# Down products of two pairs of pages at once, and a new order of loads ahead of a layer's first x

## The chip, the cores and the metric

The kernel runs on one core of a Trainium2 chip. A core has a matrix engine (TensorE, PE in the profile; its weight loads are PEld), three engines that work on rows of numbers (VectorE or DVE, ScalarE or ACT, GpSimd or POOL), and SyncE (SP), which issues transfers. ACT and POOL issue transfers too, in the order of their own instructions. Each engine goes through its own queue in order, and waits there for semaphores that other engines or transfers raise. All transfers share 16 DMA engines. The metric is device microseconds from start to end of one execution; lower is better. All arithmetic here is in 32-bit floats but for a few helpers.

## The reference, cut to what matters

An input x of 4 x 1024 tokens of width 256 goes through four residual steps: RWKV attention, a mixture of experts, retention, and the same mixture again with the same weights.

```python
x = x + attn_a(layernorm(x), ...)      # RWKV
x = x + ffn(layernorm(x), router_w, router_bias, wg, wu, wd, swg, swu, swd)
x = x + attn_b(layernorm(x), ...)      # retention, 16 heads
x = x + ffn(layernorm(x), router_w, router_bias, wg, wu, wd, swg, swu, swd)
```

The mixture takes, for each token, 4 of 64 experts, and adds two shared ones that see every token:

```python
_, topk_idx = jax.lax.top_k(logits + router_bias, K)          # K = 4, E = 64
g = jax.nn.silu(jnp.einsum('nd,edf->nef', flat, wg))          # d = 256, f = 64
u = jnp.einsum('nd,edf->nef', flat, wu)
routed = jnp.einsum('ne,nef,efd->nd', comb, g * u, wd)
shared = jnp.einsum('nsh,shd->nd', sg * su, swd)
return (routed + shared).reshape(b, t, d)
```

## The kernel before, in words

The 4096 tokens are 8 segments of 512 (NSEG, SEG). Only the chosen experts' products are computed. For that, each token's normalised row is sent four times (L429, an indirect DMA by POOL) into `sent`, a table in DRAM that is cut into pages of 128 rows. A page belongs to one expert; `owner` says to which. Two pages make a pair. As long as the tokens spread as usual, the list USUAL says how many pairs hold all rows of the segments up to i: 33, 38, 43, 51, 59, 67, 75, 83. So each of the two mixture layers (objects `f1` and `f2`) works on 83 pairs, numbered 0 to 82.

`routed` (from L520) does a pair in steps, and step p of the layer calls them for different pairs:

- `load(p)`: reads the owners of the pair, loads x, 256 KB from `sent` (L530, tile rx), and the two experts' weights, 192 KB each from `wx` (L532, tile rw), all issued on SP.
- `up(p - 2)`: four transposes of x on PE (rt, L542) and one copy on DVE (rxT, L546).
- `mid(p - 3)`: eight matmuls for gate and up (rg, L554), Silu on ACT (rs, L559), the product on DVE (rh, L562), and ACT's copy of rh to the other 64 partitions (L563), so that both halves of the down product can read it.
- `down(p - 4)`: eight matmuls (rp, L574) into two PSUM banks, one for each half of the 256 columns, two evictions of 128x256 into ry (L581), and one write of 256 KB to `made` in DRAM (L582), issued on ACT. Pairs below 33 have the second half evicted by DVE, the others by ACT.

The buffers: rx and rw four deep in layer 1 and six in layer 2, ry two and four, rh two. The tags A, B and C of the PSUM banks have 4, 3 and 1 buffers; rt, rp and some others share B.

`gather` takes the products of a segment back: 16 indirect DMAs by POOL (gy, L606; 4 tiles of 128 tokens by 4 choices), and for each an addition on DVE, weighted by the router (L617). `gathers` puts a segment's fetches at the position until(i) + 3.5, spread over 8 steps, and its additions LAG = 7 steps later. A fetch names the rows of `made` that it may read: tile t of segment i reads up to pair until(i) + 2 t, and therefore waits for the writes of all pairs before that.

All work is written out as tracks of steps with positions, which `merge` (L54) sorts into one program order; the engines' queues follow from it. Positions of layer 1 count in pairs.

The stages: `stage_1` (to about 384 us) is RWKV, the routing of layer 1 and its sends. `first_layer` (from L1184) merges layer 1's routed pairs with retention (`stage_2`, from L824), four batches of 1024 tokens, the first from position until(0) + 14 = 47. When `stage_2` is called, it issues retention's loads: five weight matrices b_w (L833), seven small vectors (L837, L840, L841), and three loads from a table of decays (L858, L865), all on SP, ahead of the first pair's loads. `stage_2`'s pools `pb` and `pw` take over memory that stage 1's pool `pa` held, with the last segment's normalised rows in it, which the sends read. After layer 1, the rest of retention and the routing of layer 2 follow, then `second_layer`: layer 2's pairs merged with gathers, the shared experts and the stores of the output (L1253).

Of the kernel before, what the change touches and what calls it, by code (L numbers as in the profile page):

```python
# [10 lines left out]
F32 = mybir.dt.float32  # L11
BF16 = mybir.dt.bfloat16
# [48 lines left out]
def hybrid_kernel(ctx: ExitStack, tc: tile.TileContext, a: dict, out: bass.AP):  # L61
# [98 lines left out]

    PACE, LAG = 2, 7.0

# [80 lines left out]
    class Ffn:  # L243
# [5 lines left out]
        def __init__(self, name, pool, keep, deep):  # L249
            self.name, self.pool, self.keep = name, pool, keep  # L250

            self.deep = deep
            self.xnT, self.pick, self.turned, self.weights = {}, {}, None, None

            self.rows = (pool, 2)

            self.paced = False


            self.end, self.room = none, None  # L260
            self.upto = self.keep.tile([P, NSEG, E], F32, tag="upto", bufs=1, name=f"upto_{name}")
# [256 lines left out]
        def routed(self, pool, until):  # L518

            st, first, last = {}, until(0), until(NSEG - 1)  # L520

            def load(p):
                nm = f"{self.name}{p}"
                _, got = nc.values_load_multi_w_load_instructions(  # L524
                    self.owner[p : p + 1, :], engines=[SP], min_val=0, max_val=E - 1,
                    skip_runtime_bounds_check_because="place() counts at most E - 1 experts",
                )
                x = pool.tile([P, 2, D], F32, tag="rx", bufs=self.deep[0], name=f"rx_{nm}")
                w = pool.tile([P, 2, WD + P], F32, tag="rw", bufs=self.deep[0], name=f"rw_{nm}")
                nc.sync.dma_start(out=x, in_=sent[p * P : (p + 1) * P])  # L530
                for j, e in enumerate(got):
                    nc.sync.dma_start(  # L532
                        out=w[:, j], in_=wx[bass.ds(e, 1)].rearrange("e p c -> p (e c)")
                    )
                st[p] = dict(x=x, w=w)

# [12 lines left out]
            def mid(p):  # L549
# [10 lines left out]

                h = pool.tile([P, 2, P], F32, tag="rh", bufs=2, name=f"rh_{nm}")
                beat(nc.vector.tensor_mul(out=h[:F], in0=gu[F:], in1=act[F:]))  # L562
                nc.scalar.copy(out=h[F:], in_=h[:F])  # L563
                s["h"] = h

            def down(p):
                nm, s = f"{self.name}{p}", st.pop(p)
                y = pool.tile([P, 2, D], F32, tag="ry", bufs=self.deep[1], name=f"ry_{nm}")
                halves = [bank("B", f"rp_{nm}_{c}", [P, 2, P]) for c in range(2)]
                for j in range(2):  # L570

                    for c, yp in enumerate(halves):
                        r = slice(c * F, (c + 1) * F)
                        nc.tensor.matmul(  # L574
                            yp[:, j, :], lhsT=s["h"][r, j, :], rhs=s["w"][r, j, WD:],
                            start=True, stop=True,
                        )
                for c, yp in enumerate(halves):

                    copy = nc.vector.tensor_copy if c and p < first else nc.scalar.copy  # L580
                    copy(out=y[:, :, c * P : (c + 1) * P], in_=yp)  # L581
                nc.scalar.dma_start(out=made[p * P : (p + 1) * P], in_=y)  # L582

            def step(p):
                if p < last:
                    load(p)
                for d, f in ((2, up), (3, mid), (4, down)):
                    if 0 <= p - d < last:
                        f(p - d)

            return track([lambda p=p: step(p) for p in range(last + 4)], 0, last + 4)

# [33 lines left out]
        def gathers(self, pool, until):  # L626

            out = []
            for i in range(NSEG):
                at = until(i) + 3.5  # L630
                fetch, add = self.gather(i, pool, until)
                out += [track(fetch, at, at + PACE * TT), track(add, at + LAG, at + LAG + PACE * TT)]
            return out


    def stage_1(ctx: ExitStack, ffn, pf):
        pa = ctx.enter_context(tc.tile_pool(name="pa", bufs=1))
        rows = ffn.rows = (pa, 4)

# [184 lines left out]
    def stage_2(ctx: ExitStack):  # L824
        pb = ctx.enter_context(tc.tile_pool(name="pb", bufs=1))
        pw = ctx.enter_context(tc.tile_pool(name="pw", bufs=2))
        NQ = T // QS
        CPQ = QS // CH

        two = [wide(n, f"b_w{n}").rearrange("p (n k d) -> p n k d", n=2, d=D) for n in range(3)]  # L830
        wq, wk, wv, wg, wo = (two[n // 2][:, n % 2] for n in range(5))
# [4 lines left out]
        for n, t in cols.items():  # L836
            nc.sync.dma_start(out=t, in_=a[n])  # L837
        bv_bc = pb.tile([P, D], F32, name="bv_bc")
        bo_3 = pb.tile([3, D], F32, name="bo_3")
        nc.sync.dma_start(out=bv_bc, in_=a["bv"].partition_broadcast(P))  # L840
        nc.sync.dma_start(out=bo_3, in_=a["bo"].partition_broadcast(3))  # L841

        bo_rows = pb.tile([3, D], BF16, name="bo_rows")
        part = pw.tile([3, D], BF16, tag="bo_part", bufs=1, name="bo_part")
        sums = pw.tile([3, D], F32, tag="bo_sums", bufs=1, name="bo_sums")
        nc.vector.memset(sums, 0.0)
# [7 lines left out]
        with nc.allow_low_precision("each row is BF16"):  # L854
            nc.vector.tensor_copy(out=bo_rows, in_=sums)

        decay = pb.tile([P, H, CH], F32, name="decay")
        nc.sync.dma_start(  # L858
            out=decay,
# [4 lines left out]
        for k in range(KC):  # L864
            nc.sync.dma_start(  # L865
                out=qdec[:, k, :],
                in_=bass.AP(
                    tensor=tab.tensor, offset=tab.offset + k * HPB * W + Z + 1,
                    ap=[[W, HPB], [0, HD], [1, CH]],
                ),  # L870
            )
# [46 lines left out]
        def normed(b, s, what):  # L918
            xnT = pw.tile([P, KC, QS], F32, tag="xnTb", bufs=1, name=f"xnT_{what}{b}_{s}")
            tiles = [xtile(b, s * CPQ + t) for t in range(CPQ)]  # L920
            xn = layernorm(pw, tiles, f"{what}{b}_{s}")
            transposed(xn, CPQ, xnT, f"{what}{b}_{s}")
# [19 lines left out]
        def batch(b):  # L942
# [7 lines left out]
            def quarter(tag, s):  # L950
                return pb.tile([P, KC, QS], F32, tag=tag, bufs=NQ + 1, name=f"{tag}_{b}_{s}")

# [210 lines left out]
    pf = ctx.enter_context(tc.tile_pool(name="pf", bufs=2))  # L1163
    f1 = Ffn("f1_", pf, keep, (4, 2, 4))

# [18 lines left out]
    def first_layer(until):  # L1184

        arm, held = ExitStack(), ExitStack()
        f2 = Ffn("f2_", pf, arm.enter_context(tc.tile_pool(name="keep2", bufs=NSEG)), (6, 4, 6))

        first = until(0) + 14
        cut = until(NSEG - 1) + 4 + LAG + PACE * TT  # L1190
        with right("pr1") as pr, right("pg") as pg:
            batch = stage_2(held)
            batches = []
            for b in range(B):
# [3 lines left out]
            merge(  # L1198
                f1.routed(pr, until), *f1.gathers(pg, until), [s for s in batches if s[0] < cut]
            )  # L1200
# [45 lines left out]
    def second_layer(f2, pr, until):  # L1246
# [5 lines left out]
        for i in range(NSEG):  # L1252
# [5 lines left out]
            f2.routed(pr, until), *gathers, stores, track(side, 0.5, n - 4),  # L1258
            track(f2.shared(NSEG - 1), n - 3, n + 4 + LAG),
        )  # L1260
# [65 lines left out]
```

## Time and profile before

| what | us |
|---|---|
| median of 3 runs | 1428.38 (1427.42 to 1430.12) |
| profiled execution, its own time | 1426.64 |
| its span, first to last instruction | 1424.7 |
| PE busy | 1260.2 (88%) |
| DVE busy | 994.2 (70%) |
| ACT busy | 738.6 (52%) |
| POOL busy | 529.9 (37%) |
| evictions of the down products on ACT (x266) | 92.8 |
| last send of layer 1 issued / first x of layer 1 issued | 381.38 / 390.59 |
| first transpose on PE, layer 1 / layer 2 | 394.93 / 1107.43 |

The transfers move 276 MB, 194 GB/s over the span, very unevenly: 349 GB/s and more between 420 and 520 us, 55 GB/s between 800 and 1074. The shares above are averages over stages with different limits. So a stage is read by the windows of the profile, which give each engine's busy time, the clock granted to PE and the DMA engines' share in one stretch; a wait, by the engine that sat idle and what released it.

### The profile page before, as it was taken

What the parts mean: (1) busy time and instruction counts of PE and PEld (TensorE: products, weight loads), DVE (VectorE), ACT (ScalarE), POOL (GpSimd) and SP (SyncE); (2) the same over time, 40 slices, a digit from 0 to 9 for tenths busy, and PEclk for the clock granted to TensorE, in tenths of its full rate; (3) what the DMA queues carried; (4) which work ended last, traced back from release to release, by engine and by line L of the source; (5) the groups of instructions that cost most, each with busy time, mean ns of one, the idle gap of its engine ahead of it and who ended that gap; (6) DMA issues with size and microseconds to landing.
All of it is one profiled execution on the core that took longest, in us unless ns stands there. A gap on an engine that the chain in (4) does not pass through costs nothing. (4 is left out here: it accounts for less than half of the span.)

```text
span 1424.7 us, 23821 instructions
## 1 busy us (share of the span) xinstructions
PE 1260.2 (88%) x7872; PEld 891.4 (63%) x7872; DVE 994.2 (70%) x2510; ACT 738.6 (52%) x1422; POOL 529.9 (37%) x536
## 2 busy tenths in 40 slices
PE   6789999999389979998998999799997899999993
PEld 2455555556277767776776666566464687777772
DVE  6999989998355547775777788866673355486664
ACT  7989888973134455555654463433331234454440
POOL 0043255536400155432334105536717000376565
PEclk9999999999789999998999999799999899999997
DMA  9985931112399996765552101212202898999984
GB/s 350 403 254 74 297 115 60 60 37 82 123 310 349 336 331 211 235 206 195 164 187 91 36 31 68 74 38 79 100 16 103 260 318 278 324 384 378 363 310 128
DMA packets 192297, 276.26 MB, mean 194 GB/s; under 512 B 53795, under 2 KB 119718, under 8 KB 192166
## 3 DMA queue, kind: packets, MB, share of 16 engines
q1 hardware_dynamic: 143686, 163.98, 36.1%
q0 software_dynamic: 24576, 67.14, 14.2%
q10 hardware_dynamic: 23904, 43.53, 8.1%
q8 instruction: 65, 1.06, 0.3%
q14 instruction: 66, 0.54, 0.1%
HBM read 166.05 MB, written 121.11 MB: 202 GB/s over the span
## 5 line engine op out<-in xcount | busy, mean ns | idle before, releaser
L429 POOL DMA_INDIRECT sent<-xn_f,to_f x256 | 278.2, 1087 | 415.3 <-issue 192.9
L606 POOL DMA_INDIRECT gy_f<-made,to_f x256 | 248.6, 971 | 468.9 <-DVE rh_f L562 143.3
L554 PE MATMUL rg_f<-rxT_f,rw_f 128*128 128x128 f32 x1328 | 186.6, 283 | 8.4 <-DVE rxT_f L546 2.9
L554 PEld LDWEIGHTS rg_f<-rxT_f,rw_f 128*128 128x128 f32 x1328 | 165.9, 194 | 19.7 <-DVE rxT_f L546 11.6
L559 ACT ACTIVATE rs_f<-rg_f 64x256 f32<-64x256 f32 x166 | 62.4, 376 | 218.9 <-PE rg_f L554 187.4
L542 PE MATMUL rt_f<-ident,rx_f 128*128 128x128 f32 x664 | 107.2, 285 | 45.3 <-DMA rx_f<-sent 41.5
L574 PE MATMUL rp_f<-rw_f,rh_f 64*128 64x128 f32 x1328 | 137.9, 300 | 6.9 <-DVE rh_f L562 3.6
L546 DVE COPY rxT_f<-rt_f 128x512 f32<-128x512 f32 x166 | 114.2, 688 | 39.5 <-PE rt_f L542 37.9
L581 ACT COPY ry_f<-rp_f 128x256 f32<-128x256 f32 x266 | 92.8, 374 | 90.8 <-DMA made<-ry_f 40.3
L617 DVE SCALAR_TENSOR_TENSOR x<-gy_f,w_f,x 128x256 f32<-128x256 f32 x256 | 122.1, 480 | 14.6 <-DMA gy_f<-made,to_f 10.8
L457 PE MATMUL g_f<-xnT_f,f_swg 128*128 128x512 f32 x256 | 130.7, 627 | 0.6 <-ACT sh_f L462 0.6
L470 PE MATMUL o_f<-f_swd,sh_f 128*128 128x256 f32 x512 | 121.5, 385 | 8.2 <-DVE sh_f L463 4.2
L574 PEld LDWEIGHTS rp_f<-rw_f,rh_f 64*128 64x128 f32 x1328 | 102.1, 186 | 34.9 <-ACT ry_f L581 8.7
L457 PE MATMUL u_f<-xnT_f,f_swu 128*128 128x512 f32 x256 | 122.2, 595 | 0.7 <-DVE sh_f L463 0.7
L542 PEld LDWEIGHTS rt_f<-ident,rx_f 128*128 128x128 f32 x664 | 76.2, 144 | 69.4 <-issue 34.1
L562 DVE TENSOR_TENSOR rh_f<-rg_f,rs_f 64x256 f32<-64x256 f32 x166 | 70.6, 426 | 64.9 <-ACT rs_f L559 61.8
L470 PEld LDWEIGHTS o_f<-f_swd,sh_f 128*128 128x128 f32 x512 | 94.9, 190 | 30.0 <-DVE sh_f L463 6.7
L683 PE MATMUL rvk<-xnT_a,rvk 128*128 128x512 f32 x192 | 91.5, 623 | 7.9 <-DVE xnT_a L240 7.4
L1060 DVE TENSOR_TENSOR pm<-sc,decay 128x512 f32<-128x512 f32 x128 | 83.8, 681 | 8.3 <-PE sc L1039 7.1
L463 DVE TENSOR_TENSOR sh_f<-u_f,sh_f 128x512 f32<-128x512 f32 x64 | 43.7, 685 | 62.5 <-PE u_f L457 56.3
L462 ACT ACTIVATE sh_f<-g_f 128x512 f32<-128x512 f32 x64 | 38.0, 596 | 90.7 <-PE g_f L457 50.9
L457 PEld LDWEIGHTS u_f<-xnT_f,f_swu 128*128 128x128 f32 x256 | 48.1, 191 | 57.1 <-issue 52.6
(238 smaller groups left out, 2178.0 us busy)
## 6 DMA issues: line engine op xcount, KB each, us to landing
rw_f<-wx SPq DMA_DIRECT2D x332, 192.0 KB
rx_f<-sent SPq DMA_DIRECT2D x166, 256.0 KB
made<-ry_f ACTq DMA_DIRECT2D x166, 256.0 KB
sent<-zeros SPq DMA_DIRECT2D x7, 2048.0 KB
sent<-zeros SPq DMA_DIRECT2D x1, 10240.0 KB
x<-in_x_dram SPq DMA_DIRECT2D x8, 512.0 KB
wx<-in_wg_dram SPq DMA_DIRECT2D x2, 2048.0 KB
sent<-xn_f,to_f POOLq DMA_INDIRECT x256
```

What stands on the lines that cost most here:

```text
L429: ins = nc.gpsimd.indirect_dma_start(out=rows_sent[: pairs_until(i) * 2 * P, :], out_offset=bass.IndirectOffsetOnAxis(ap=st["to"][:, c : c ...
L457: nc.tensor.matmul(ps, lhsT=w[:, k, s], rhs=self.xnT[i][:, k, :], start=(k == 0), stop=(k == KC - 1),)
L470: nc.tensor.matmul(o[:, t, :], lhsT=st["h"][:, c, s], rhs=self.weights[2][:, c, :], start=(c == 0), stop=(c == NS - 1),)
L542: nc.tensor.transpose(tp[:, k, j, :], s["x"][:, j, k * P : (k + 1) * P], ident)
L546: beat(nc.vector.tensor_copy(out=xT, in_=tp))
L554: nc.tensor.matmul(gu[:, j, :], lhsT=s["w"][:, j, k * 2 * F : (k + 1) * 2 * F], rhs=s["xT"][:, k, j, :], start=(k == 0), stop=(k == KC - 1),)
L574: nc.tensor.matmul(yp[:, j, :], lhsT=s["h"][r, j, :], rhs=s["w"][r, j, WD:], start=True, stop=True,)
L581: copy(out=y[:, :, c * P : (c + 1) * P], in_=yp)
L606: ins = nc.gpsimd.indirect_dma_start(out=got[t][:, k, :], out_offset=None, in_=rows_made[: ready[t] * 2 * P, :], in_offset=bass.IndirectOf ...
L617: tc.keep_in_program_order(nc.vector.scalar_tensor_tensor(out=xs[i][:, t, :], in0=got[t][:, k, :], scalar=s["w"][:, c : c + 1], in1=xs[i][ ...
L683: nc.tensor.matmul(ps, lhsT=rvk[:, k, lo : lo + P], rhs=st["xnT"][:, k, :], start=(k == 0), stop=(k == KC - 1),)
L1060: ins = nc.vector.tensor_mul(out=pm, in0=ch[j]["sc"][g], in1=decay.rearrange("p (k g b) n -> p g k b n", k=KC, b=2)[:, g],)
```

## The change

It has four parts.

Down products: `down` takes two neighbouring pairs, an even one and the odd one behind it. Each of the two PSUM banks holds one half of the columns for both pairs ([P, 2, 2, P], 512 floats per partition) and is evicted once (128x512), and one transfer of 512 KB writes both pairs to `made`. It runs in the step in which the odd pair's down product ran before. Pair 82, the last, is done alone. The ry buffers are two of double size in both layers, and rh has three buffers for two. Fetches of a segment start one step later where until(i) is odd, but for the last segment; the additions come 5 steps after the fetches in layer 1 (7 before) and 7 in layer 2. The gy buffers go from 4 to 3 in layer 1 and from 6 to 5 in layer 2.

Weights: a function of its own loads a pair's weights, with five rw buffers in layer 1 and seven in layer 2; `begin` loads the first five or seven pairs' weights before any x. In layer 1 it runs before `stage_2` issues its loads.

Retention's small loads: the seven vectors and three loads from the decay table are issued on ACT instead of SP. The b_w loads stay on SP, behind the first weights.

Memory: stage 1's normalised rows have a pool of their own, opened first; `stage_2` has three pools that wait for the earlier holder of each tile's memory alone, with `decay` placed first, one buffer for its normalised rows, and two helpers in the buffers of other tiles. Retention's first batch starts at until(0) + 13 = 46.

```diff
 class Ffn:
     def __init__(self, name, pool, keep, deep):
-            self.deep = deep
+            *self.deep, self.lag = deep
...
-            def load(p):
+            def load_weights(p):
...
-                x = pool.tile([P, 2, D], F32, tag="rx", bufs=self.deep[0], name=f"rx_{nm}")
-                w = pool.tile([P, 2, WD + P], F32, tag="rw", bufs=self.deep[0], name=f"rw_{nm}")
-                nc.sync.dma_start(out=x, in_=sent[p * P : (p + 1) * P])
+                w = pool.tile([P, 2, WD + P], F32, tag="rw", bufs=self.deep[3], name=f"rw_{nm}")
                 for j, e in enumerate(got):
                     nc.sync.dma_start(
                         out=w[:, j], in_=wx[bass.ds(e, 1)].rearrange("e p c -> p (e c)")
                     )
+            def begin():
+                for p in range(min(self.deep[3], last)):
+                    load_weights(p)
+
+            def load(p):
+                x = pool.tile(
+                    [P, 2, D], F32, tag="rx", bufs=self.deep[0], name=f"rx_{self.name}{p}"
+                )
+                nc.sync.dma_start(out=x, in_=sent[p * P : (p + 1) * P])
+                if p >= self.deep[3]:
+                    load_weights(p)
+                st[p]["x"] = x
...
-                h = pool.tile([P, 2, P], F32, tag="rh", bufs=2, name=f"rh_{nm}")
+                h = pool.tile([P, 2, P], F32, tag="rh", bufs=3, name=f"rh_{nm}")
...
-            def down(p):
+            def down(ps):
+                p, n = ps[0], len(ps)
+                nm = f"{self.name}{p}"
+                y = pool.tile([P, 2, 2, D], F32, tag="ry", bufs=self.deep[1], name=f"ry_{nm}")
+                halves = [bank("B", f"rp_{nm}_{c}", [P, 2, 2, P]) for c in range(2)]
+                for u in range(n):
+                    s = st.pop(p + u)
+                    for j in range(2):
+                        for c, yp in enumerate(halves):
+                            r = slice(c * F, (c + 1) * F)
+                            nc.tensor.matmul(
+                                yp[:, u, j, :], lhsT=s["h"][r, j, :], rhs=s["w"][r, j, WD:],
+                                start=True, stop=True,
+                            )
                 for c, yp in enumerate(halves):
                     copy = nc.vector.tensor_copy if c and p < first else nc.scalar.copy
-                    copy(out=y[:, :, c * P : (c + 1) * P], in_=yp)
-                nc.scalar.dma_start(out=made[p * P : (p + 1) * P], in_=y)
+                    copy(out=y[:, :n, :, c * P : (c + 1) * P], in_=yp[:, :n])
+                nc.scalar.dma_start(
+                    out=made[p * P : (p + n) * P].rearrange("(u p) j d -> p u j d", p=P),
+                    in_=y[:, :n],
+                )

             def step(p):
                 if p < last:
                     load(p)
-                for d, f in ((2, up), (3, mid), (4, down)):
+                for d, f in ((2, up), (3, mid)):
                     if 0 <= p - d < last:
                         f(p - d)
-            return track([lambda p=p: step(p) for p in range(last + 4)], 0, last + 4)
+                q = p - 4
+                if 0 <= q < last and (q % 2 or q == last - 1):
+                    down(range(q - q % 2, q + 1))
+            return [(-1, begin)] + track([lambda p=p: step(p) for p in range(last + 4)], 0, last + 4)
...
-                at = until(i) + 3.5
+                at = until(i) + 3.5 + (until(i) % 2 if i + 1 < NSEG else 0)
...
     def stage_1(ctx: ExitStack, ffn, pf):
+        pn = ctx.enter_context(tc.tile_pool(name="pn", bufs=1))
+        rows = ffn.rows = (pn, 4)
         pa = ctx.enter_context(tc.tile_pool(name="pa", bufs=1))
-        rows = ffn.rows = (pa, 4)
...
     def stage_2(ctx: ExitStack):
-        pb = ctx.enter_context(tc.tile_pool(name="pb", bufs=1))
-        pw = ctx.enter_context(tc.tile_pool(name="pw", bufs=2))
+        pq = ctx.enter_context(tc.tile_pool(name="pq", bufs=1, reuse_waits="tile"))
+        pb = ctx.enter_context(tc.tile_pool(name="pb", bufs=1, reuse_waits="tile"))
+        pw = ctx.enter_context(tc.tile_pool(name="pw", bufs=2, reuse_waits="tile"))
...
         for n, t in cols.items():
-            nc.sync.dma_start(out=t, in_=a[n])
+            nc.scalar.dma_start(out=t, in_=a[n])
...
-    f1 = Ffn("f1_", pf, keep, (4, 2, 4))
+    f1 = Ffn("f1_", pf, keep, (4, 2, 3, 5, 5.0))
...
-        f2 = Ffn("f2_", pf, arm.enter_context(tc.tile_pool(name="keep2", bufs=NSEG)), (6, 4, 6))
-        first = until(0) + 14
+        f2 = Ffn("f2_", pf, arm.enter_context(tc.tile_pool(name="keep2", bufs=NSEG)), (6, 2, 5, 7, 7.0))
+        first = until(0) + 13
...
+            pairs = f1.routed(pr, until)
+            pairs.pop(0)[1]()
             batch = stage_2(held)
```

## The prediction

> **What bounds the kernel now.** I read the profile in this order: the windows (which engine is full in which stage), the timeline where layer 1's routed pairs begin, the chain of waits on the engines those pairs use, and the timeline of the end. The windows first; the columns are the stretch, its length, busy time of PE, its weight loads, DVE, ACT and POOL, then granted clock, share of the DMA engines, GB/s:
>
> ```profile
> 362.00:384.00 22.00, 7.66 (x34) 5.76 (x32) 2.84 (x9) 0.13 (x1) 14.50 (x17) 0.80 0.47 155
> 384.00:404.00 20.00, 8.11 (x41) 7.06 (x42) 8.00 (x22) 1.64 (x5) 1.23 (x5) 0.54 0.70 211
> 440.00:460.00 20.00, 19.36 (x157) 16.02 (x159) 11.56 (x24) 9.06 (x24) 0.00 (x0) 1.00 1.01 349
> 523.00:800.00 277.00, 261.25 (x2115) 203.33 (x2116) 194.35 (x482) 148.87 (x319) 103.48 (x107) 0.97 0.56 179
> 1118.00:1230.00 112.00, 112.00 (x834) 89.20 (x833) 59.49 (x116) 45.50 (x116) 3.52 (x4) 1.00 0.90 295
> 1230.00:1365.00 135.00, 129.63 (x921) 100.89 (x920) 88.99 (x175) 62.93 (x166) 85.71 (x89) 0.99 1.03 372
> 1392.00:1424.00 32.00, 9.06 (x37) 6.57 (x35) 15.20 (x31) 0.60 (x1) 17.46 (x18) 0.72 0.41 125
> ```
>
> From 404 to about 520 the DMA engines are full (1.01 at 349 GB/s). From 523 on PE is the bound (261 of 277 us busy), in layer 2 as well. Two places have neither: 362 to 404, and the end, which is POOL's row of fetches. The first of them in the timeline:
>
> ```profile
> 381.38 0.96 POOL L429 DMA_INDIRECT sent<-xn_f,to_f  x1 [0.30 <-DMA sent<-xn_f,to_f]
> 383.93 0.35 SPq L837 DMA_DIRECT2D b_bq<-in_bq_dram  x1
> 387.52 3.03 SPq L865 DMA_DIRECT2D qdec<-tab  x2
> 390.59 0.45 SPq L530 DMA_DIRECT2D rx_f<-sent  x1
> 392.07 1.32 SPq L532 DMA_DIRECT2D rw_f<-wx  x2
> 394.93 1.09 PE L542 MATMUL rt_f<-ident,rx_f 128*128 128x128 f32 x4 [24.49 <-DMA rx_f<-sent]
> ```
>
> The last send has landed at 383.9. Retention's small loads waited for it on SP and are issued until 390.6, and only then comes the first x. The waits that bear on the pairs:
>
> ```profile
> PE rt_f L542 <- DMA rx_f<-sent: 41.5, 15, 24.5
> ACT ry_f L581 <- DMA made<-ry_f: 40.3, 34, 2.7
> ACT rh_f L563 <- DVE rh_f L562: 22.0, 39, 2.3
> ```
>
> **The change part by part.** (a) Order at the start of layer 1. In the changed program SP issues five pairs' weights and the five b_w loads right behind the last owner (ready at 362.6), with nothing in front of x0 that waits for the sends; retention's small loads stand on ACT, and wait for no send. SP needs about 2.2 us for a pair (rx issues at 1107.78 and 1110.02 in layer 2), so five pairs and five b_w (0.5 each) end near 376, ahead of 383.9. ACT's share of the move is about 6.7 us of issuing (383.93 to 390.59) in a wait of 37.7 us before its first rs; if that cover were gone it would cost at most those 6.7. x0 then goes out at 383.9 instead of 390.59; in layer 2 the step from rx's issue to PE takes 2.6 (1104.81 to 1107.43), so PE starts at 386.6 instead of 394.9: -8.2 us. What is late next is the send itself. Ends: -8.2 and, if the sends land later beside the new neighbours, -3. I take -8.2, since 3.41 MB moved in 362 to 384 and 1.97 MB more make 245 GB/s there, below the 349 of a full stretch.
>
> The Trainium skill's page DMA: Bandwidth & Descriptors (section Issuing engines are not separate DMA queues) says that issuing from several engines saves only the sequencer's issue time, usually small beside the transfer. The trace agrees with the first half, not the second: that issue time is 6.7 us here and the x load behind it takes 2.6. If it were small, the term would be about -1.5 and the sum 1425.
>
> (b) Weights ahead. 5 x 393,216 B = 1.97 MB move out of the full stretch: 1.97 MB / 349 GB/s = -5.6 us. Ends: 0 (if a loop and not bytes sets the 2.63 us per pair; made's issues go from 417.5 to 496.4 in 30 pairs) and -9 (rival 2). A pair moves 917,504 B, and 917,504 B / 349 GB/s = 2.63 us, exactly the pace, so I take the bytes.
>
> (c) Paired down products. Same matmuls. Evictions: 332 of 128x256 (374 ns on ACT, 425 on DVE) become 168, of 128x512 but for two a layer; the nearest rows, transposed activations, give 584 and 679 ns. ACT loses about 20 us of work and half of its 166 issues of 0.33 us, 27 us; ACT is 52% busy and off the path, so 0. Layer 1's two ry buffers become two of double size (four pairs), layer 2's four singles two doubles of the same bytes; if the wait on made goes, what is late next is the full DMA: 0, ends 0 and -9, the latter rival 2.
>
> (d) A new wait. Down of the odd pair needs that pair's copy of rh, which in the new order of ACT stands behind the next pair's Silu in 24 of 41 groups of layer 1 and 15 of 41 of layer 2. Behind PE's waiting rp stand the next pair's transposes; ACT's eviction and through it the write wait for rp. An exact row doesn't exist; a Silu of 376 ns less what PE does between gives about 0.3 us. In the full-DMA stretches that is slack. Ends: 0 and (15 + 5) x 0.3 = +6; some of layer 2's groups lie where the DMA is full too (1.03): +2.
>
> (e) Layer 2's start. Before, rt0 is at 1107.43, rt1 waits for its x until 1110.64, and rg0 is at 1112.40, since each x stood behind two weight issues. Now seven pairs' weights are there (their SP issues lie between the owners, 1077, and the sends' end, 1104, in a wait of 37.4 us) and the x loads go out back to back: rg0 after two groups of 1.1 us, at 1109.6: -2.8. Ends -4 and 0.
>
> (f) Middle. Batch 0 starts one pair earlier, adds come two steps earlier and the fetches one later, with three gy buffers for four. The first fetch waits for pairs 32 and 33, written together: about 3 us later. It is to be added one step (3.3 us) earlier than before (508.85), and its slack goes from some 9 us to 2. 0, ends -4 and +4. The small memsets and tables of stage 2 are off the path (before 523), 0.
>
> (g) The end. The lines of before, POOL and ACT's queue:
>
> ```profile
> 1388.85 0.94 POOL L606 DMA_INDIRECT gy_f<-made,to_f  x1 [1.31 <-DMA made<-ry_f]
> 1392.85 0.95 POOL L606 DMA_INDIRECT gy_f<-made,to_f  x1 [0.30 <-issue]
> 1395.78 1.17 POOL L606 DMA_INDIRECT gy_f<-made,to_f  x1 [1.99 <-DMA made<-ry_f]
> ```
>
> ```profile
> 1390.67 0.33 ACTq L582 DMA_DIRECT2D made<-ry_f  x1
> 1391.83 0.33 ACTq L582 DMA_DIRECT2D made<-ry_f  x1
> ```
>
> Segment 6's last four fetches (from 1388.85) need pair 80. It was written by itself at 1385.0; now it goes with pair 81, at about 1390.7, and lands 4 to 4.6 us later, near 1395. So four fetches that lay ahead of the last write come behind it: 4 x 1.27 (1.25 to 1.5 each) = 5.1, less the 0.6 by which they may start before 1395.78: +4.5. Ends +1 and +6.
>
> Sum: -8.2 - 5.6 + 0 + 2 - 2.8 + 0 + 4.5 = -10.1. The profiled execution took 1426.64 us (span 1424.7), which gives 1416.5; it lies 1.7 below the median of the runs shown, 1428.38, and from that the sum gives 1418.3. I take 1418.
>
> **The rivals.** 1: the weights ahead bring nothing, because the pace is the loop of buffers (ry_f waits 40.3 us for made). Then the sum is -4.5: 1424. For it: the first four pairs run at 2.38 us while the DMA is as busy. Against: bytes over rate give the pace to the digit.
>
> 2: that loop was the limit and is gone, and the full stretch runs at the 384 to 387 GB/s seen in 500 to 520. A pair is then 2.38 us instead of 2.63; over 35 pairs -8.8: 1409.5. Against: the write queue already moves 6.02 MB in 26.3% of 60 us (420 to 480), 381 GB/s of its own time; reads, which don't change, make 336.
>
> The same page of the Trainium skill (section Bandwidth) gives 138 GB/s at 64 KB and 341 at 1 MB, so it would have the 512 KB writes run better; no run here shows a write of that size yet.
>
> 3, slower: paired downs stall PE in its own stretches. Without (d) the sum is -12.1, and 2.9 us, 0.2% (about what a measurement of this kernel tells from no change), lie beyond zero. PE-bound groups are 20 in layer 1 and 41 in layer 2, so it decides from 15 / 61 = 0.25 us a group on. If each waits for one rh copy of 0.40 us, that is +24: 1440. For it: ACT's copy already waits 22.0 us for DVE. Against: most groups of layer 2 have the copy ahead of the Silu, and PE has rt and rg of later pairs in front of rp.
>
> 4: the starts are early but the lead isn't kept in the merged stretch (f), whose fetches have 2 us of slack. Only (d), (e), (g) and nothing else remain: +3.7, 1432; with half the lead, 1425. Against: PE is 94% busy from 523 to 800, so an early start is kept.
>
> **How the numbers follow.** Forecast 1418 with 0.42, its own range 1412 to 1423; rival 1 0.16; rival 2 0.18; rival 3 0.12; rival 4 0.12 (0.06 slower, 0.03 the same, 0.03 faster). Of the forecast and rival 1, 0.04 end within 0.2% by costs at their upper ends. So faster 0.42 + 0.16 + 0.18 + 0.03 - 0.04 = 0.75, same 0.07, slower 0.18. The range goes from 1407, a little under rival 2, to 1432, with about 0.1 left out on each side.
>
> **What would show it.** x0 issued at about 384 and PE at 386 to 387; weights ahead between 363 and 376; batch 0's start about 14 us earlier; rg0 in layer 2 within 5 us of x0's issue; gaps of PE before the odd pair's rp no longer than 0.3 us; four fetches of segment 6 behind the last pair's write. Wrong would be: sends that land after 386, pace per pair in the full stretch away from 2.63, DVE waiting for fetches near 510 to 545, or PE's gaps before rp in most groups.

## The result, and the profile after

The changed kernel took 1412.71 us (median of 4, 1409.69 to 1421.3) against 1429.25 (1427.42 to 1432.59): a ratio of 0.989, 95% interval 0.985 to 0.993. The forecast was 1418, faster. Its profiled execution took 1409.69 us with a span of 1408.0, so the two traces differ by 16.7 us of span. The forecast's steps don't add up to that in the way they were meant to: some are as forecast, one brought nothing, and the stretch for which a cost was forecast holds the largest gain.

The two traces, cut at the same events (the last owner of a layer, its last send, first matmuls of pairs, the first transpose of batch 0, the last down product):

| stretch | before | after | difference | forecast |
|---|---|---|---|---|
| start to the last owner of layer 1 | 362.8 | 359.2 | -3.6 | 0 |
| last owner to the first rg (a) | 34.1 | 28.3 | -5.8 | -8.2 |
| first rg to rg of pair 5 | 13.6 | 11.4 | -2.2 | |
| pair 5 to pair 35 (b, c) | 79.4 | 87.2 | +7.8 | -5.6 for all three |
| pair 35 to batch 0 | 33.9 | 30.1 | -3.8 | |
| batch 0 to the last owner of layer 2 (f) | 553.6 | 551.5 | -2.2 | 0 |
| last send of layer 2 to its first rg (e) | 10.1 | 7.1 | -3.0 | -2.8 |
| first rg to the last rp of layer 2 (d) | 278.4 | 270.7 | -7.7 | +2 |
| last rp to the last segment's fetches (g) | 4.9 | 8.9 | +4.0 | +4.5 |

What is left out (the sends of layer 2, the end behind the fetches) differs by 0.2 us together. The first row holds nothing that was edited; in later traces the same stage took 379 to 395 us, so its 3.6 us are not ascribed to the change. And batch 0 now starts one pair earlier in the program's order, so most of the 3.8 us from pair 35 to batch 0 is that one pair (2.9 us at the pace of pairs 5 to 35).

The start of layer 1 in the changed kernel, from its timeline on POOL, SP and PE:

```profile
377.80 0.96 POOL L430 DMA_INDIRECT sent<-xn_f,to_f  x1 [0.30 <-issue]
360.30 13.72 SPq L531 DMA_DIRECT2D rw_f<-wx  x10
374.12 0.40 SPq L863 DMA_DIRECT2D b_w<-in_wq_dram  x1
382.78 7.97 SPq L545 DMA_DIRECT2D rx_f<-sent  x7
385.53 1.94 PE L555 MATMUL rt_f<-ident,rx_f 128*128 128x128 f32 x8 [18.67 <-DMA rx_f<-sent]
```

Weights and b_w are out by 376.7, as forecast. The x loads follow each other with nothing between, and PE starts 2.75 us behind the first. But x goes out 5.0 us behind the last send, where the first small load of before went out 2.55 behind it: the sends land 2.4 us later beside their new neighbours.

The windows of the changed kernel (columns as in the prediction) for layer 1's start, pairs 5 to 35, and the first third of layer 2, and below them two of its waits in pairs 5 to 35 (total, times, longest):

```profile
382.00:399.00 17.00, 13.45 (x101) 12.51 (x102) 9.78 (x21) 4.87 (x12) 0.00 (x0) 0.73 0.64 192
399.00:486.00 87.00, 71.81 (x597) 62.22 (x596) 42.54 (x75) 30.08 (x74) 0.00 (x0) 0.94 0.93 312
1104.00:1160.00 56.00, 56.00 (x436) 46.20 (x435) 29.99 (x53) 21.18 (x49) 0.00 (x0) 1.00 0.85 280
```

```profile
DVE rxT_f L559 <- PE rt_f L555: 26.6, 18, 3.9
PE rt_f L555 <- DMA rx_f<-sent: 9.9, 10, 1.9
```

The stretch that was full (1.01 at 349 GB/s) is no longer: 0.93 at 312 GB/s, with PE waiting 9.9 us for x (1.5 in the same pairs before). In layer 2 PE is busy without a gap (56.00 of 56 us), so there the length of its own blocks decides. The wait of ry for the write is gone, as rival 2 had it, but the rate fell instead of rising. A lead of 5.8 us at the first rg, counted from the last owner, has grown to 8.0 at pair 5 and is 0.2 at pair 35. So all that the start and the weights ahead gained in layer 1 was used up by pair 35.

### The profile page after: what moved, and what is told of

Its sections match the earlier page's. It is cut to its first block, busy times and chain, and to the rows that moved or that the text cites. A ratio compares the mean times of both kernels' runs of the same rounds, so it can differ in the third digit from the quotient of the medians.

```text
span 1408.0 us, 23163 instructions
## 1 busy us (share of the span) xinstructions
PE 1233.3 (88%) x7872; PEld 884.0 (63%) x7872; DVE 989.2 (70%) x2476; ACT 714.5 (51%) x1291; POOL 528.1 (38%) x536
## 4 chain that ended last, share of the span: by engine, by line
PE 45%; DVE 26%; DMA 9%; ACT 8%; issue 6%; POOL 4%; SPq 1%; POOLq 0%; ACTq 0%; DVEq 0%
PE rg_f L567 7%; PE rp_f L591 5%; PE g_f L458 4%; PE rt_f L555 3%; PE o_f L471 3%; PE u_f L458 3%; DVE pm L1089 3%; PE rp L1110 3%; DMA made<-ry_f 2%; PE op L1176 2%; DMA rx_f<-sent 2%; DVE x L640 2%; POOL sent L430 2%; POOL gy_f L629 2%; PE k L965 2%
## 5 line engine op out<-in xcount | busy, mean ns | idle before, releaser
L567 PE MATMUL rg_f<-rxT_f,rw_f 128*128 128x128 f32 x1328 | 189.6, 285 | 17.6 <-DVE rxT_f L559 10.9
L458 PE MATMUL g_f<-xnT_f,f_swg 128*128 128x512 f32 x256 | 126.3, 609 | 0.6 <-ACT sh_f L463 0.6
L591 PE MATMUL rp_f<-rw_f,rh_f 64*128 64x128 f32 x1328 | 119.3, 294 | 8.1 <-DVE rxT_f L559 3.2
L591 PEld LDWEIGHTS rp_f<-rw_f,rh_f 64*128 64x128 f32 x1328 | 97.3, 191 | 25.3 <-DVE rxT_f L559 3.7
L576 ACT COPY rh_f<-rh_f 64x256 f32<-64x256 f32 x166 | 66.5, 401 | 79.8 <-DVE rh_f L575 79.3
L598 ACT COPY ry_f<-rp_f 128x512 f32<-128x512 f32 (+1 forms) x134 | 73.4, 582 | 21.9 <-PE rp_f L591 20.1
```

Of the source, the lines that this page charges most:

```text
L458: nc.tensor.matmul(ps, lhsT=w[:, k, s], rhs=self.xnT[i][:, k, :], start=(k == 0), stop=(k == KC - 1),)
L567: nc.tensor.matmul(gu[:, j, :], lhsT=s["w"][:, j, k * 2 * F : (k + 1) * 2 * F], rhs=s["xT"][:, k, j, :], start=(k == 0), stop=(k == KC - 1),)
L591: nc.tensor.matmul(yp[:, u, j, :], lhsT=s["h"][r, j, :], rhs=s["w"][r, j, WD:], start=True, stop=True,)
L598: copy(out=y[:, :n, :, c * P : (c + 1) * P], in_=yp[:, :n])
```

## The experiments

The experiments fell on three chips, numbered 0, 5 and 15, where the kernel before took 1582 to 1602 us. In their traces engines also wait 143 to 251 us in all for a releaser outside the core, of which the first two traces show nothing. So each ratio is against the kernel before on the same chip, and the mechanisms are read from stretches in which no trace has such a wait: pairs 5 to 35 of both layers, and the time from the last rp to the last segment's fetches. The changed kernel itself ran again on chip 0 alone.

### The changed kernel again

> The changed kernel itself, beside the next three: the runs above fell on a chip whose kernel before took 1588 us, so each part is set against the changed kernel on one chip. If the first comparison holds (0.989): layer 1 from pair 5 to 35 in about 87 us, layer 2 from rg0 to pair 35 in about 108.5, the end as it was.

On this chip (0) it is not faster than the kernel before: 0.9995 (0.996 to 1.003). Pairs 5 to 35 took 90.4 us, layer 2's pairs 5 to 35 the same 91.3 us as in the first trace, the end 10.1. So the 1.1% is no property of the kernel alone. Part of what is different shows on SP in layer 2: the seven pairs' weights took 12.1 us to issue in the first trace and 29.5 here, so the first x stood behind them and left 12.4 us behind the last send instead of 2.4. In that same time other engines wait:

```profile
DVE sh_f L464 <- remote: 19.1, 1, 19.1
ACT sh_f L463 <- remote: 9.3, 1, 9.3
```

(Waits of the changed kernel on that chip, 1226 to 1250 us.) What "remote" is can't be told from the trace.

### Down products pair by pair

```diff
-    f1 = Ffn("f1_", pf, keep, (4, 2, 3, 5, 5.0))
+    f1 = Ffn("f1_", pf, keep, (4, 4, 3, 5, 5.0, 1))
...
-                y = pool.tile([P, 2, 2, D], F32, tag="ry", bufs=self.deep[1], name=f"ry_{nm}")
+                y = pool.tile([P, self.group, 2, D], F32, tag="ry", bufs=self.deep[1], name=f"ry_{nm}")
...
+                if self.group == 1:
+                    down(range(q, q + 1))
```

The last number is `self.group`, 1 in both layers here; with 1, the fetches have no extra step.

> The changed kernel with down products pair by pair in both layers (ry four singles, one write of 256 KB per pair, fetches without the extra step). Theory 1 (a block of 16 down matmuls costs PE 0.2 us a pair less where PE is the bound; in layer 1's full stretch pairing costs about 8 us, because it lets the weights' buffers go in twos): the stretch from pair 5 to 35 back from 87 to about 79 us, layer 2's pairs 8 us slower, the end 3.5 us earlier, in all 1410 to 1418. Theory 2 (as in the prediction: paired downs change nothing but waits and the end; the start gives the gain): stretch unchanged at 87, layer 2 unchanged, the end 3.5 earlier, in all about 1409 with PE's time per pair as in the changed kernel.

> Down products pair by pair in both layers, again, beside the changed kernel. Theory 1 (pairing costs in layer 1's full stretch, wins on PE): pairs 5 to 35 about 4 to 8 us quicker than in the changed kernel, layer 2 from rg0 to pair 35 about 4 slower, over all pairs 8, the end 3.5 earlier; totals within 5 us of each other. Theory 2 (pairing costs nothing in the stretch): the stretch alike within 1 us.

It has the lowest ratio on both of its chips: 0.992 (0.987 to 0.997) on chip 5, and 0.979 (0.972 to 0.986) on chip 0 beside the changed kernel's 0.9995. Pairs 5 to 35 took 83.6 and 81.3 us, the latter beside the changed kernel's 90.4. Layer 2's pairs 5 to 35 took 94.7 against 91.3, to the hundredth the same in both of its traces, and the last segment's fetches began 4.7 us behind the last rp, against 8.2 to 10.1. Theory 1 holds in all three; theory 2 falls. Its totals were too low for theory 1 though: in the stretch of retention, from batch 0 to layer 2's last owner, it took 621 and 626 us (the two kernels that pair in layer 2 alone took 623) against 628 to 646 in the changed kernel and its variants that pair in layer 1. Neither theory had that, and since this stretch holds waits for outside the core, its cause stays open.

The windows of the stretch on chip 0, with single downs and in the changed kernel:

```profile
437.00:518.00 81.00, 70.31 (x595) 58.66 (x594) 44.54 (x89) 33.94 (x90) 0.00 (x0) 0.98 0.98 335
```

```profile
427.00:517.00 90.00, 72.21 (x595) 62.79 (x593) 42.45 (x75) 30.12 (x75) 0.00 (x0) 0.92 0.91 300
```

The matmuls are the same; the DMA engines' share is 0.98 against 0.91, at 335 against 300 GB/s.

### Pairing in layer 2 alone

```diff
-    f1 = Ffn("f1_", pf, keep, (4, 2, 3, 5, 5.0))
+    f1 = Ffn("f1_", pf, keep, (4, 4, 3, 5, 5.0, 1))
...
+        f2 = Ffn("f2_", pf, arm.enter_context(tc.tile_pool(name="keep2", bufs=NSEG)), (6, 2, 5, 7, 7.0, 2))
```

> The changed kernel with pairing in layer 2 alone. Theory 1: layer 1's stretch as in the kernel with single downs (79 us), layer 2 as in the changed kernel (rg0 to the last rp about 271 us), in all about 1405 if the 8 us of the stretch reach the end, 1412 if the merged stretch with retention takes them back. Theory 2: as the changed kernel, 1412.

0.9946 (0.990 to 0.999), against 0.9919 for single downs on the same chip: no difference that counts. Pairs 5 to 35 of layer 1 took 85.0 us, those of layer 2 91.3. The 3.4 us that layer 2 gains there don't show in the total. The end alone lost 5.1 us (fetches 9.8 us behind the last rp, against 4.7), and the later pairs hold waits for outside the core.

### Paired downs alone

> The kernel before with the paired downs alone (rh three, ry doubled, gy 3 and 5, fetches one step later); queues and loads as before. Theory 1: start as before (x0 9.2 us behind the last send), layer 1's stretch slower than 79 us, layer 2's pairs 8 us faster, the end 3.5 later: 1422 to 1430. Theory 2: nothing gained, the end later: 1432 to 1434.

The kernel before with `down(ps)` of the change, its buffers and its later fetches: 1.0275 (1.018 to 1.037), slower than either theory had. It is not the paired downs alone: it has the change's three gy buffers with the old distance of 7 steps between fetch and addition, which the change shortens to 5. So the total says that pairing without the rest is a loss here, and not how much of it is pairing's.

One part can be told, ahead of the first fetch: pairs 5 to 35 took 101.7 us, where the kernel before took 79.4 on its chip and the changed kernel without weights ahead (next section) 87.8 on this one. In the code of these pairs it differs from the latter in its four rw buffers for five. Its window of the stretch, and what SP waited for there:

```profile
436.00:538.00 102.00, 72.52 (x605) 59.95 (x601) 43.92 (x75) 30.53 (x75) 0.00 (x0) 0.97 0.83 271
SPq L532 <- PE rp_f L578: 23.2, 16, 2.7
```

SP waited 23.2 us for down products to let go of weights' buffers, about once for each group of two pairs (9.6 us in 19 waits in the kernel before). With four buffers, two of which come free at once, the loads stop for that time.

### No weights ahead

```diff
             def begin():
-                for p in range(min(self.deep[3], last)):
-                    load_weights(p)
+                pass
...
-                if p >= self.deep[3]:
-                    load_weights(p)
+                load_weights(p)
```

> The changed kernel without weights ahead: each pair's weights are issued behind its x, in both layers. By the prediction the bytes come back into the full stretch: layer 1 5.6 us slower, rg0 of layer 2 2.8 later, in all about 1421. By the rival (the stretch is no longer full, so bytes moved out of it are worth little): layer 1 at most 2 us slower by pair 35, in all about 1415 to 1417.

1.0011 (0.997 to 1.005). The first x left 2.46 us behind the last send, 1.3 to 3.0 us sooner than in the paired kernels with weights ahead on these chips (3.7 to 5.4, the one with the small loads on SP left aside), and the first rg came 25.8 us behind the last owner instead of 28.3. Pairs 0 to 5 were slower by 1.8 (13.2 against 11.4), and by pair 35 it stood at 126.8 us from the last owner, the changed kernel in its two traces at 126.9 and 131.2, its variants with five buffers at 122 to 133. So the rival holds as far as single traces tell: bytes moved out of a stretch that is no longer full bring nothing that shows at pair 35, and the price is the sends' landing. In layer 2, too, rg came 16.4 us behind the last send, against 18.2 to 22.0 in the paired kernels with weights ahead on these chips.

### Retention's small loads on SP again

```diff
-            nc.scalar.dma_start(out=t, in_=a[n])
+            nc.sync.dma_start(out=t, in_=a[n])
```

(and the other loads alike; the pools as changed.)

> The changed kernel with retention's small loads on SP again, behind the weights and b_w and ahead of the first x; they no longer wait for the sends there. If the queue is what counted (the 6.7 us of issuing): x0 issued 3 to 6 us later than in the changed kernel, in all 3 to 6 us slower. If the wait for the sends was what counted (the memory): SP is through with them before the sends have landed, x0 at most 1 us later, in all unchanged.

SP's timeline of this kernel:

```profile
379.93 13.30 SPq L531 DMA_DIRECT2D rw_f<-wx  x10
401.04 0.00 SPq L867 DMA_DIRECT2D b_bq<-in_bq_dram  x1
403.77 3.00 SPq L894 DMA_DIRECT2D qdec<-tab  x2
406.87 7.02 SPq L545 DMA_DIRECT2D rx_f<-sent  x6
```

The last send left at 397.5. The small loads didn't wait for it, but they stand behind the weights, and SP got to them at 401.0 and to x 5.8 us later: 9.4 us behind the last send, as in the kernel before (9.2), against 4.3 in the changed kernel on this chip. The queue counts, with nearly the 6.7 us that the prediction gave it. The total can't be told from that of the changed kernel, 0.999 against 0.9995: of the 5 us at x 2 were left at pair 35 (133.3 against 131.2 from the last owner), and 2 us of 1600 lie within these intervals. An early start that runs into a slower stretch is worth less than it measures.

### Two writes, and the old evictions under the new order

Two writes of 256 KB instead of one of 512:

```diff
-                nc.scalar.dma_start(
-                    out=made[p * P : (p + n) * P].rearrange("(u p) j d -> p u j d", p=P),
-                    in_=y[:, :n],
-                )
+                for u in range(n):
+                    nc.scalar.dma_start(out=made[(p + u) * P : (p + u + 1) * P], in_=y[:, u])
```

> The changed kernel, each pair of pairs still in one eviction per half, but written with two transfers of 256 KB. If the size of the write is what slows layer 1's stretch: pairs 5 to 35 back to 79 to 82 us from 87. If it is the order (two pairs' weights let go at once, and loads in bursts): 87 as before, and totals alike within 2 us.

And the same with four evictions of 128x256 for two pairs, so that only PE's order is left of the pairing:

```diff
-                    copy(out=y[:, :n, :, c * P : (c + 1) * P], in_=yp[:, :n])
+                    for u in range(n):
+                        copy(out=y[:, u, :, c * P : (c + 1) * P], in_=yp[:, u])
```

> The changed kernel with PE's order kept (16 down matmuls of two pairs in one block, into the same two banks), but four evictions of 128x256 and two writes of 256 KB for two pairs, as many as before. If PE's gain comes from the order of its blocks alone: layer 2 from pair 5 to 20 in 42.8 us and from 20 to 35 in 48.4, as in the changed kernel (45.4 and 49.3 with single downs). If it comes from the wider evictions: 45.4 and 49.3. Layer 1 from pair 5 to 35 in 86 to 90 if order and release of buffers slow it, 81 to 84 if eviction or write size do.

The first: 0.9947 (0.991 to 0.998), where the changed kernel beside it has 0.9995 (0.996 to 1.003), so the totals are not told apart; pairs 5 to 35 took 85.9 us, against 90.4 in the changed kernel on that chip, between the two answers. The second, on chip 15: 0.9978 (0.993 to 1.003), 83.8 us, where paired downs with wide evictions and writes took 88.2 (x a step earlier, below) and single ones 80.0 (the last experiment). By what was expected, that speaks for eviction or write size as a part of layer 1's loss; single traces of one order differ by as much. In layer 2 the second took 42.84 and 48.44 us, those of the changed kernel to the hundredth. So PE's gain comes from the order of its blocks alone, and the wide evictions add nothing to it. PE's timeline of a pair and more with single downs (kernel before), and of two pairs in this one, which here follow a shared expert's matmuls:

```profile
1142.29 0.66 PE L542 MATMUL rt_f<-ident,rx_f 128*128 128x128 f32 x4
1142.78 1.06 PE L554 MATMUL rg_f<-rxT_f,rw_f 128*128 128x128 f32 x8
1143.77 0.72 PE L574 MATMUL rp_f<-rw_f,rh_f 64*128 64x128 f32 x8
1144.41 0.66 PE L542 MATMUL rt_f<-ident,rx_f 128*128 128x128 f32 x4
```

```profile
1296.18 0.60 PE L555 MATMUL rt_f<-ident,rx_f 128*128 128x128 f32 x4
1296.61 1.06 PE L567 MATMUL rg_f<-rxT_f,rw_f 128*128 128x128 f32 x8
1297.51 0.60 PE L555 MATMUL rt_f<-ident,rx_f 128*128 128x128 f32 x4
1297.94 1.06 PE L567 MATMUL rg_f<-rxT_f,rw_f 128*128 128x128 f32 x8
1298.93 1.16 PE L591 MATMUL rp_f<-rw_f,rh_f 64*128 64x128 f32 x16
```

By start times, a pair with single downs takes 0.49 + 0.99 + 0.64 = 2.12 us. For two with paired downs it is 0.49 (rt behind rp; 0.43 in the line above, behind the shared expert) + 0.90 + 0.43 + 0.99 and a block of 16 down matmuls, 1.09 by the median of such blocks ahead of rt: 3.90, or 1.95 a pair. The same eight rg matmuls take 0.90 us ahead of rt and 0.99 ahead of rp. So the blocks shrink where a change between matmuls over 64 rows (rp) and over 128 (rt, rg) has gone: 4.24 less 3.90 is 0.34 us for two changes out of four.

The Trainium skill's page TensorEngine Tiling (Array Packing), section Key Properties, says that changing the tiling mode drains the engine. The trace fits that, at about 0.17 us for a change.

Not every block of 16 takes 1.09 us. In the changed kernel's first trace, two of layer 2's blocks and ACT's copy of the odd pair's rh for each:

```profile
1130.48 1.56 PE L591 MATMUL rp_f<-rw_f,rh_f 64*128 64x128 f32 x16
1130.87 0.40 ACT L576 COPY rh_f<-rh_f 64x256 f32<-64x256 f32 x1
1137.85 1.16 PE L591 MATMUL rp_f<-rw_f,rh_f 64*128 64x128 f32 x16
1137.49 0.40 ACT L576 COPY rh_f<-rh_f 64x256 f32<-64x256 f32 x1 [0.49 <-DVE rh_f L575]
```

The tenth matmul of a block is the first to read that copy. In the second block the copy was there 0.5 us before it, and the block took 1.09 us to the start of the next. In the first it ended 0.14 us behind that matmul's start, the starts behind it are spread, and the block took 1.49. So it is in 15 of layer 2's 41 groups (1.47 to 1.49 us), the very ones whose copy stands behind the next pair's Silu on ACT. Pairs 5 to 35 hold 15 groups, five of them late in this way: 15 x 0.34 - 5 x 0.40 = 3.1 us, where 3.4 were measured. This is the new wait of the prediction's part (d). No row of waits shows it, since PE's record has no idle time there; the start times do.

### A sixth buffer of weights, and x a step earlier

```diff
-    f1 = Ffn("f1_", pf, keep, (4, 2, 3, 5, 5.0))
+    f1 = Ffn("f1_", pf, keep, (4, 2, 2, 6, 5.0))
```

> The changed kernel with six weights' buffers instead of five in layer 1 (and gy two instead of three, which pays for them and acts from pair 37 on). If layer 1's stretch is slow since two pairs' weights are let go at once and too few loads are under way: pairs 5 to 35 down from 86 to 90 us to 82 or less, DMA share up from 0.92 to 0.97 or more. If the depth of weights has no part in it: 86 to 90. After pair 37 it may lose by gy.

```diff
             def load(p):
+                for n in range(1 if p else 0, 2):
+                    if p + n < last:
+                        load_x(p + n)
+                if p >= self.deep[3]:
+                    load_weights(p)
+                st[p]["x"] = x_of.pop(p)
+
+            def load_x(p):
                 x = pool.tile(
...
-                if p >= self.deep[3]:
-                    load_weights(p)
-                st[p]["x"] = x
+                x_of[p] = x
```

> The changed kernel with each x issued one step earlier on SP, ahead of the weights of the pair before, with the same four rx buffers. If x loads are late because they stand behind weights that wait for the paired downs (PE's rt waited 9 to 10 us for x in this stretch): pairs 5 to 35 in 82 us or less, the wait of rt for x under 4 us. If the rate and not the order of the loads is short: 86 to 90 and the wait moves to rg on weights.

With six buffers pairs 5 to 35 took 84.3 us with a DMA share of 0.94: between the two answers, and by itself no proof. Beside the paired downs alone it is one end of a row: 101.7 us with four buffers, 87.2 to 90.4 with five, 84.3 with six. With x ahead they took 88.2, and the wait moved as the second answer had it. Its waits in the stretch:

```profile
PEld rg_f L575 <- DMA rw_f<-wx: 12.0, 13, 2.6
PE rg_f L575 <- DMA rw_f<-wx: 10.3, 13, 2.3
PE rt_f L563 <- DMA rx_f<-sent: 1.0, 3, 0.4
```

PE waits 1.0 us for x and 10.3 for weights, where it waited 8.9 and 5.6 in the changed kernel (on the other chip). So it isn't the order of the two loads. In all: 0.996 (0.991 to 1.001) and 1.001 (0.996 to 1.006).

### Layer 1 single, layer 2 paired but for its last three pairs

```diff
+                if self.group == 1 or (self is not f1 and q >= last - 3):
+                    down(range(q, q + 1))
```

(the rest as in the kernel with pairing in layer 2 alone.)

> Layer 1 with single downs, layer 2 paired but for its last three pairs. From the runs so far: layer 1 from pair 5 to 35 in 81 to 85 us, layer 2's pairs 5 to 35 in 91.3 (94.7 with single downs), from the last rp to the last segment's fetches 4.7 to 5 us instead of 9 to 10. In all 4 to 10 us less than the changed kernel on the same chip; if the last pair's write and not segment 6's fetches set the end, no change there.

0.9964 (0.992 to 1.001). Pairs 5 to 35 of layer 1 took 80.0 us with a DMA share of 0.99, layer 2's 91.3, and the fetches of the last segment began 7.2 us behind the last rp: better than 8.2 to 10.1, not the 4.7 of single downs. It was built to join the gains of both, and each stretch shows its gain. But the changed kernel did not run on this chip, so the 4 to 10 us are not shown, and no kernel here has a lower ratio than single downs throughout (on other chips).

## Why the prediction was right or wrong

The time lies in its range and 5 us under its value; the terms deserve less credit than the sum.

(a) The start: right in its mechanism, mis-sized. -5.8 of -8.2; the missing 2.4 are the sends that land later beside the weights ahead (a wait of 5.0 us behind the last send for 2.55). The prediction had this as the other end of its range, and set it aside because 245 GB/s lie below 349. The run without weights ahead shows it: x at 2.46 us behind the last send, on another chip.

(b) Weights ahead: wrong. The step was "a pair moves 917,504 B, and 917,504 B / 349 GB/s = 2.63 us, exactly the pace, so I take the bytes". That is a fact of the kernel before and holds only as long as the stretch stays full. The same change made it 2.91 us a pair at 312 GB/s, and then bytes moved out of it bring nothing that shows: without weights ahead pair 35 stands where it stood. Rival 1 had this outcome for another reason: the loop of ry buffers that it named was gone.

(c) The paired downs: "0, ends 0 and -9" had the wrong sign. In layer 1 the pairing cost some 3 to 9 us of pairs 5 to 35, chip by chip: 83.6 and 85.0 us single against 87.8 paired, 81.3 against 87.9 and 90.4, 80.0 against 88.2. The transfers moved 326 to 341 GB/s there with single downs, and 300 to 317 with paired ones. The part that I had left out is the weights: a pair's weights are in use until its down product, so pairing lets go of two at once and later. With four buffers pairs 5 to 35 took 101.7 us, SP waiting 23.2 us for down products, and 14 us less with a fifth on the same chip. What is left with five may also have to do with the larger writes and evictions (85.9 and 83.8 with narrow ones; a sixth buffer gives 84.3, x ahead nothing). How it is shared is open, since single traces of one order differ by up to 5 us (80.0 to 85.0 with single downs). The trace of before already held eight writes of 512 KB, the stores of the output, which the prediction's remark on that size passed over.

(d) The new wait: right as a wait, and a term was missing beside it. In layer 2 it came in 15 of 41 groups, as many as the prediction had counted, with 0.4 us in each where 0.3 was the estimate: about 6 us, the upper end of its range, where +2 was taken. In 10 of the 15 the copy began within 0.04 us of the end of DVE's product, so there it was the product that came late, and not the Silu that stood in front. PE's row of waits for rh, 1.2 us in the whole trace, hides all this. The stretch gained 7.7 us all the same, since PE's blocks shrink with fewer changes between 64 and 128 rows: 41 groups at 0.34 us are 14, less 6 is 8 (an estimate from the blocks above). "Same matmuls" in part (c) was the failing step: I priced matmuls as equal because their number was. Rows of before spoke against it, for rt took 0.49 us behind rp and 0.43 behind a shared expert's matmuls. The Trainium skill's sentence on draining, cited above, spoke for this gain and was overlooked. Rival 3 had the stall right and the sign of the whole wrong.

(e) and (g) held on the first chip: -3.0 for -2.8, and +4.0 for +4.5. On the other chips (e) turned round: with weights ahead rg0 of layer 2 came 18.2 to 22.0 us behind the last send, in the run without them 16.4. The fetches of segment 6 that wait for pair 80, and then the last segment's, in the changed kernel's POOL timeline:

```profile
1371.52 0.95 POOL L629 DMA_INDIRECT gy_f<-made,to_f  x1 [0.30 <-issue]
1374.11 0.94 POOL L629 DMA_INDIRECT gy_f<-made,to_f  x1 [1.64 <-DMA made<-ry_f]
1379.23 1.07 POOL L629 DMA_INDIRECT gy_f<-made,to_f  x1 [0.30 <-issue]
```

The write of pairs 80 and 81 is issued at 1369.67, lands 4.4 us later, and four fetches of 1.28 us go ahead of the sixteen that end the kernel.

(f) The middle: 0 was forecast, -2.2 came; within its bounds.

So the sum was near because two errors met. From the last owner to batch 0, -13.8 was forecast and -4.0 came; in layer 2's pairs, +2 was forecast and -7.7 came. These cancel by luck, and of the remaining 6.6 us (16.7 for 10.1) 3.6 lie in a stage that was not edited, 2.2 in the middle.

## What to carry to other kernels

A rate read off a full stretch is a price for bytes only while the change leaves the stretch full; when the same change also alters how buffers are let go, ask first whether loads are still under way all the time. Grouping matmuls of one form saves PE the changes between forms, 0.17 us each here, and can be had without wider evictions or writes; but the second half of a group must not run into operands that are not ready yet, 0.4 us each time here. Such a wait can hide inside a busy block: compare start times of like blocks, and not the idle time alone. A pairing of outputs delays whoever waits for the first of the two: look at the last consumer, here sixteen fetches in a row, and at the buffers that the first of the two keeps.

## What the runs showed of the hardware

A change of PE between matmuls over 64 and over 128 rows cost about 0.17 us (3.90 against 4.24 us for the same 40 matmuls of two pairs; the evictions and writes are of the same size in the two kernels compared). A block of 16 matmuls that ran into an operand 0.14 us late took 0.40 us longer, with no idle time in PE's record. On three chips the kernel before took 11 to 12% longer, and the changed kernel 14% on one of them. Engines waited there for a releaser outside the core, in one case 19.1 us while the seven pairs' weights were loaded. On that chip the gain of the changed kernel was gone: a margin of 1% can belong to the chip on which it was found.
